# Layer 2's pairwise factor made once per pair of row tiles, in one arena of buffers

## The chip, the cores and the metric

The kernel runs on one core of one Trainium2 chip. The metric is the device time of one execution in microseconds. A core has five engines that work beside each other, each with its own queue of instructions in a fixed order: TensorE (PE, matrix products into the accumulation memory PSUM), VectorE (DVE), ScalarE (ACT, functions by tables), GpSimd (POOL) and SyncE (SP, here the issuer of DMA transfers). They meet through semaphores.

## The reference

Four graph layers run one after the other on 2708 nodes with 128 features. Each layer's output is added to its input and normalised. The change touches layer 2, a layer in hyperbolic space. Cut to what matters there:

```python
def logmap(p1, p2):
    sub = mobius_add(-p1, p2)
    sn = _norm(sub)
    return 2.0 / (sc * lambda_x(p1)) * artanh(sc * sn) * sub / sn

x = proj(x)
h = proj(mobius_matvec(W, x))
h = proj(mobius_add(h, proj(expmap0(b[None, :]))))
h_t = logmap0(h)
local_t = logmap(h[:, None, :], h[None, :, :])          # all pairs of nodes
scores = h_t @ att_wl
scores = scores[:, None] + (h_t @ att_wr)[None, :] + att_b[0]
adj_att = jax.nn.sigmoid(scores) * adj
support_t = jnp.einsum('ij,ijd->id', adj_att, local_t)
h = proj(expmap(support_t, h))
```

Each pair of nodes needs one scalar of the distance kind: with c the hyperbolic cosine of the pair's distance, the factor is arccosh(c) / sinh. This factor is the same for (i, j) and (j, i). The attention weight (sigmoid times adjacency) is not.

## The kernel before

The 2708 nodes are cut into NT = 22 row tiles of 128 (the last has 20 rows). All state lies in SBUF. Layers 0 and 1 take the time up to about 1180 us, the preparation of layer 2 to about 1242, the pairs of layer 2 from there to about 1617, then the end of layer 2 and the two adjacency products of layer 3.

The pairs are computed transposed: a unit (hf, j) has the 128 source nodes of row tile j on the partitions and half of all target nodes on the columns. There are two halves, hf = 0 with HW = 1408 columns (HT = 11 tiles) and hf = 1 with 1300. So there are 44 units, worked in the order of j, first half first. One unit goes through these steps (method names of class Pair, lines of the profile):

- load (L1330): SP brings the adjacency tile `at`. If the diagonal lies in it, POOL multiplies a 128 x 128 part by `off` to clear it (L1335).
- gram (L1337): PE makes products of the node vectors in float32 (L1343) and adds a correction of ten bfloat16 rows (L1344), 512 columns at a time into a PSUM buffer `ps`. ACT clears it into `m` (relu of minus, L1348); in every third unit DVE does this (L1346). `m` is c - 1.
- square (L1350), root (L1355), log (L1366): ACT makes u = (m + 1)^2, r = 1 / sqrt(u - 1), and later the logarithm.
- sinh (L1360), exp_d (L1363): DVE makes u = (u - 1) r, the sinh, and m = m + 1 + u, whose logarithm is the distance.
- gate (L1369), gated_adj (L1374): ACT makes the sigmoid of the scores, DVE multiplies it by `at`.
- times_d (L1377), over_sinh (L1380): DVE multiplies the distance by the gated adjacency and by r.
- add_up (L1383): PE adds the unit's part to `accV` (L1391, 128 rows) and to `accO` (L1393, one row per 512 columns, in three column groups of the array), which stay in PSUM over all 22 units of a half. After a half's last unit they are copied out. The first half's result goes to DRAM (`v_tab`) and is read again at layer 3's start, the second's stays in `VT1`.

Square and relu need no table change on ACT. Root, log and sigmoid are in three tables, so ACT loads three tables in each step.

Units go in trios, G = 3. One step of the loop handles `now` (roots, sinh, log, products), `after` (the next trio: loads, grams, squares, gates) and `done` (the previous trio: add_up). The order within a step is written out by hand under `tc.manual_schedule()`, and each engine keeps it:

```python
for v in now: v.root()
for v in now: v.gated_adj()
for v in after: v.load()
for v in now: v.sinh()
add_up(0); gram(after, 1)
for v in now: v.exp_d()
for v in after[:2]: v.square()
add_up(1); gram(after, 2)          # its clears are on DVE
for v in now: v.log()
for v in after[2:]: v.square()
for v in now: v.times_d()
for v in after: v.gate()
add_up(2); gram(trio(step + 2), 0)
for v in now: v.over_sinh()
```

The buffers come from five pools: 7 for m, 5 for u, 4 each for r, w and `at`, all of 1408 columns. Grams use a pool of four PSUM buffers.

Of the kernel before, what the change touches and what calls it, by code (L numbers as in the profile page):

```python
# [3 lines left out]

# [8 lines left out]
F32 = mybir.dt.float32  # L13
BF16 = mybir.dt.bfloat16
U32 = mybir.dt.uint32
AF = mybir.ActivationFunctionType
# [4 lines left out]
P = 128  # L21
# [18 lines left out]
def gnn_stack(ctx: ExitStack, tc: tile.TileContext, t, out: bass.AP):  # L40
# [975 lines left out]
    def layers_1_to_3(top, before_end=lambda: None):  # L1016
# [144 lines left out]
        with ExitStack() as l2:  # L1161
# [139 lines left out]
            HT = NT // 2  # L1301
            HW = HT * P
            halves = [(0, HW), (HW, N)]
            assert all(b - a <= 3 * BANK for a, b in halves)
            G = 3
            V0T = wp.tile([P, 2, BANK], F32, name="V0T")
            nc.vector.memset(V0T, 0.0)
            with ExitStack() as att:
                pm = att.enter_context(tc.tile_pool(name="pair_m", bufs=2 * G + 1))
                pu = att.enter_context(tc.tile_pool(name="pair_u", bufs=2 * G - 1))  # L1310
                pr = att.enter_context(tc.tile_pool(name="pair_r", bufs=G + 1))
                pw = att.enter_context(tc.tile_pool(name="pair_w", bufs=G + 1))
                stream = att.enter_context(tc.tile_pool(name="adj2", bufs=G + 1))
                pacc = att.enter_context(tc.tile_pool(name="ps_acc2", bufs=1, space=PSUM))
                pg = att.enter_context(tc.tile_pool(name="ps_g", bufs=4, space=PSUM))

                class Pair:

                    acc = {}

                    def __init__(self, hf, j):
                        self.hf, self.j, self.r = hf, j, rows[j]
                        self.c0, self.c1 = halves[hf]
                        self.w = self.c1 - self.c0
                        self.js = slice(j * P, j * P + self.r)

                    def new(self, pool, name):
                        return pool.tile([P, HW], F32, name=name)[:self.r, :self.w]

                    def load(self):  # L1330
                        self.at = self.new(stream, "at")
                        nc.sync.dma_start(out=self.at, in_=adjT[self.js, self.c0:self.c1])
                        if self.c0 <= self.j * P < self.c1:
                            d = self.at[:, self.j * P - self.c0:self.j * P - self.c0 + self.r]
                            nc.gpsimd.tensor_mul(d, d, off[:self.r, :self.r])  # L1335

                    def gram(self, on_vector):  # L1337

                        self.m = self.new(pm, "m")
                        for a, b in spans(0, self.w, BANK):  # L1340
                            ps = pg.tile([P, BANK], F32, name="ps")[:self.r, :b - a]
                            c = slice(self.c0 + a, self.c0 + b)
                            nc.tensor.matmul(ps, XT[:, self.js], XT[:, c], start=True, stop=False)  # L1343
                            nc.tensor.matmul(ps, aux[0][:, self.js], aux[1][:, c], start=False, stop=True)  # L1344
                            if on_vector:
                                nc.vector.tensor_scalar(self.m[:, a:b], ps, -1.0, 0.0, op0=ALU.mult, op1=ALU.max)  # L1346
                            else:
                                nc.scalar.activation(self.m[:, a:b], ps, AF.Relu, scale=-1.0)  # L1348

                    def square(self):  # L1350

                        self.u = self.new(pu, "u")
                        nc.scalar.activation(self.u, self.m, AF.Square, bias=1.0)

                    def root(self):  # L1355

                        self.r_ = self.new(pr, "r")
                        nc.scalar.activation(self.r_, self.u, AF.Abs_reciprocal_sqrt, bias=less[:self.r])

                    def sinh(self):  # L1360
                        nc.vector.scalar_tensor_tensor(self.u, self.u, LESS_ONE, self.r_, op0=ALU.add, op1=ALU.mult)  # L1361

                    def exp_d(self):  # L1363
                        nc.vector.scalar_tensor_tensor(self.m, self.m, 1.0, self.u, op0=ALU.add, op1=ALU.add)  # L1364

                    def log(self):  # L1366
                        nc.scalar.activation(self.m, self.m, AF.Ln)

                    def gate(self):  # L1369
                        self.w_ = self.new(pw, "w")  # L1370
                        nc.scalar.activation(self.w_, slB[:self.r, self.c0:self.c1], AF.Sigmoid,
                                             bias=sr[:self.r, self.j:self.j + 1])

                    def gated_adj(self):  # L1374
                        nc.vector.tensor_mul(self.w_, self.w_, self.at)  # L1375

                    def times_d(self):  # L1377
                        nc.vector.scalar_tensor_tensor(self.m, self.m, DMAX, self.w_, op0=ALU.min, op1=ALU.mult)  # L1378

                    def over_sinh(self):  # L1380
                        nc.vector.tensor_mul(self.m, self.m, self.r_)  # L1381

                    def add_up(self):  # L1383
                        first, last = self.j == 0, self.j == NT - 1
                        if first:
                            Pair.acc = (pacc.tile([P, 3 * BANK], F32, name="accV"),
                                        pacc.tile([P, BANK], F32, name="accO"))
                        accV, accO = Pair.acc
                        pieces = spans(0, self.w, BANK)
                        for a, b in pieces:  # L1390
                            nc.tensor.matmul(accV[:, a:b], X[:self.r, self.j, :], self.m[:, a:b], start=first, stop=last)  # L1391
                        for k, (a, b) in enumerate(pieces):
                            nc.tensor.matmul(accO[32 * k:32 * k + 1, :b - a], X0[:self.r, self.j:self.j + 1],  # L1393
                                             self.m[:, a:b], start=first, stop=last)
                        if last:
                            VT = VT1 if self.hf else pr.tile([P, HW], F32, name="r")[:, :self.w]
                            for k, (a, b) in enumerate(pieces):
                                copy = nc.scalar.copy if k % 2 else nc.vector.tensor_copy
                                copy(VT[:, a:b], accV[:, a:b])
                                copy(V0T[32 * k:32 * k + 1, self.hf, :b - a], accO[32 * k:32 * k + 1, :b - a])  # L1400
                            if self.hf == 0:
                                nc.sync.dma_start(out=v_tab, in_=VT)

                units = [Pair(hf, j) for hf in range(2) for j in range(NT)]
                trios = [units[n:n + G] for n in range(0, len(units), G)]

                def trio(n):
                    return trios[n] if 0 <= n < len(trios) else []

                with tc.manual_schedule():
                    for v in trio(0):
                        v.load()
                    for step in range(-1, len(trios) + 1):
                        now, after, done = trio(step), trio(step + 1), trio(step - 1)

                        def add_up(n):
                            for v in done[n:n + 1]:  # L1420
                                v.add_up()

                        def gram(vs, n):
                            for v in vs[n:n + 1]:
                                v.gram(n == 2)

                        if step < 0:
                            gram(after, 0)
                        for v in now:
                            v.root()  # L1430
                        for v in now:
                            v.gated_adj()
                        if step >= 0:
                            for v in after:
                                v.load()
                        for v in now:
                            v.sinh()
                        add_up(0)
                        gram(after, 1)
                        for v in now:  # L1440
                            v.exp_d()
                        for v in after[:2]:
                            v.square()
                        add_up(1)
                        gram(after, 2)
                        for v in now:
                            v.log()
                        for v in after[2:]:
                            v.square()
                        for v in now:  # L1450
                            v.times_d()
                        for v in after:
                            v.gate()
                        add_up(2)
                        gram(trio(step + 2), 0)
                        for v in now:
                            v.over_sinh()

# [276 lines left out]
```

## Time and profile before

| What | us |
|---|---|
| median of three runs (1917.05 to 1921.48) | 1919.34 |
| span of the profiled execution, first to last instruction | 1917.7 |
| PE busy in the whole span | 1659.6 |
| DVE busy | 1542.7 |
| ACT busy | 1132.0 |
| POOL busy | 680.1 |
| first clear of a gram, layer 2 | at 1242.6 |
| last add_up of layer 2 ends | at 1616.6 |
| start of layer 3's first adjacency product | at 1672.4 |

The profile gives one execution. Its own time outside the profiler is not given apart from the span; the median of the runs lies 1.6 us above the span. Shares over the whole span mix stages with different limits, so the stretch from 1242 to 1618 is to be read by itself. In a group a matrix product in float32 appears as two records, and the end of a record is modelled, so the pitch from one start to the next is the better price.

### The profile page before, as it was taken

The numbers are of one execution on the slowest core, as the hardware profiler recorded it, in microseconds if no ns is written. First come the engines' busy times: TensorE is split into PE (matmuls) and PEld (weight loads), VectorE is DVE, ScalarE is ACT, GpSimd is POOL, SyncE is SP. The second block draws the span as 40 slices with busy tenths as digits, with TensorE's granted clock in tenths as the row PEclk, the third lists the DMA queues.
The fourth block names the chain that finished last, engine by engine and source line by source line (L and its number), as shares of the span: only waits on it lengthen the run. The fifth ranks groups of instructions, "written<-read, shape, count | busy, mean of one in ns | idle before, by whom it ended". The sixth has DMA issues, their size and how long they took to land.

```text
span 1917.7 us, 36464 instructions
## 1 busy us (share of the span) xinstructions
PE 1659.6 (87%) x13973; PEld 949.3 (50%) x13973; DVE 1542.7 (80%) x3632; ACT 1132.0 (59%) x1581; POOL 680.1 (35%) x426
## 2 busy tenths in 40 slices
PE   5899999999999999885699996689998996199995
PEld 4666666666666666664444443322222322044542
DVE  7899999999999999986588885789999997760104
ACT  3566666667666666654344444599998994440003
POOL 5667757767766776664100000022000243000000
PEclk8899999999999999997799997779998997599997
DMA  8756566665666666443044410122222212453330
GB/s 223 161 117 148 121 140 143 132 143 119 148 127 133 146 128 142 91 103 109 1 151 149 170 63 1 61 91 91 78 80 70 98 63 120 161 203 145 139 127 31
DMA packets 218839, 223.63 MB, mean 117 GB/s; under 512 B 28389, under 2 KB 204875, under 8 KB 212067
## 3 DMA queue, kind: packets, MB, share of 16 engines
q1 hardware_dynamic: 167614, 197.53, 33.1%
q0 software_dynamic: 51040, 23.68, 10.5%
q8 instruction: 111, 1.82, 0.4%
q14 instruction: 74, 0.60, 0.1%
HBM read 213.33 MB, written 7.83 MB: 115 GB/s over the span
## 4 chain that ended last, share of the span: by engine, by line
DVE 37%; PE 32%; POOL 10%; issue 7%; ACT 7%; DMA 6%; SPq 0%; DVEq 0%; ACTq 0%; POOLq 0%
PE acc L1634 10%; POOL far L781 9%; PE lg L1098 5%; PE acc L1105 5%; DVE ix L777 5%; DMA far<-d_tab,ix 3%; DVE w L1375 3%; DVE u L1361 3%; DVE m L1364 3%; DVE W L882 3%; PE sl L817 2%; DVE extra L795 2%; DVE m L1381 2%; DVE o L739 2%; DVE m L1378 2%
## 5 line engine op out<-in xcount | busy, mean ns | idle before, releaser
L781 POOL DMA_INDIRECT far<-d_tab,ix x352 | 562.3, 1597 | 259.5 <-DVE W L882 110.8
L895 ACT ACTIVATE g<-sl 128x768 f32<-128x768 f32 x484 | 393.4, 813 | 259.0 <-PE sl L822 240.5
L817 PE MATMUL sl<-dA,S 124*128 124x153 f16 x4840 | 409.0, 232 | 10.4 <-DVE W L882 8.0
L817 PEld LDWEIGHTS <-S 124*128 124x128 f16 x4840 | 331.0, 98 | 80.0 <-issue 68.4
L833 PE MATMUL acc<-g,W 128*32 128x128 f32 x4840 | 206.2, 278 | 0.5 <-DVE W L882 0.5
L1335 POOL TENSOR_TENSOR at<-at,off 128x128 f32<-128x128 f32 (+1 forms) x22 | 71.2, 3249 | 328.8 <-DMA at<-in_adjT 301.2
L833 PEld LDWEIGHTS acc<-g,W 128*32 128x32 f32 x4840 | 140.9, 109 | 58.7 <-issue 54.6
L822 PE MATMUL sl<-s,same 50*128 50x384 f16 x968 | 162.0, 308 | 0.0
L1391 PE MATMUL accV<-m,X 128*128 128x512 f32 (+4 forms) x264 | 128.4, 628 | 33.5 <-DVE m L1381 29.1
L882 DVE TENSOR_TENSOR W<-sl,own 128x150 f32<-128x150 f32 x484 | 143.1, 299 | 14.5 <-ACT g L895 14.2
L1099 ACT ACTIVATE w<-lg,row_L_gnn_gate_bias 128x512 f32<-128x512 f32 (+1 forms) x132 | 83.5, 636 | 108.2 <-PE lg L1098 106.9
L1343 PE MATMUL ps<-XT 128*128 128x512 f32 (+4 forms) x264 | 143.9, 629 | 3.8 <-ACT m L1348 3.6
L707 DVE TENSOR_SCALAR S<-rk 124x1000 f16<-124x1000 bf16 (+1 forms) x330 | 133.4, 430 | 0.0
L777 DVE FIND_INDEX8 ix<-v,o 128x8 uint32<-128x2728 f32 x44 | 131.7, 2993 | 0.0
L316 DVE TENSOR_TENSOR g<-ps,row_L_gnn_b 128x512 f32<-128x512 f32 (+2 forms) x14 | 7.9, 574 | 148.3 <-PE ps L314 148.2
L1098 PE MATMUL lg<-qT,mT 128*128 128x512 f32 (+2 forms) x264 | 121.1, 547 | 3.6 <-ACT w L1099 3.1
L1105 PE MATMUL acc<-w,both 128*128 128x512 f32 (+2 forms) x264 | 121.2, 547 | 0.0
L795 DVE SCALAR_TENSOR_TENSOR extra<-far,v,extra 128x128 f32<-128x128 f32 x330 | 114.8, 348 | 6.3
L739 DVE SCALAR_TENSOR_TENSOR o<-ps,ar 128x496 f32<-128x496 f32 x132 | 82.4, 624 | 38.1 <-PE ps L728 31.7
L1634 PE MATMUL acc<-at,x 128*128 128x512 f32 (+2 forms) x156 | 66.2, 574 | 48.8 <-ACT x L246 48.8
L1100 DVE TENSOR_TENSOR w<-w,at 128x512 f32<-128x512 f32 (+1 forms) x132 | 82.5, 625 | 27.2 <-ACT w L1099 27.1
L1391 PEld LDWEIGHTS accV<-m,X 128*128 128x128 f32 (+1 forms) x264 | 52.1, 211 | 97.0 <-issue 57.7
(358 smaller groups left out, 2697.6 us busy)
## 6 DMA issues: line engine op xcount, KB each, us to landing
at<-in_adjT SPq DMA_DIRECT2D x42, 1354.0 KB
ar<-in_adj SPq DMA_DIRECT2D x105, 248.0 KB
far<-s_tab SPq DMA_DIRECT2D x44, 512.0 KB
at<-in_adjT SPq DMA_DIRECT2D x42, 448.0 KB
at<-in_adjT SPq DMA_DIRECT2D x21, 704.0 KB
at<-in_adjT SPq DMA_DIRECT2D x21, 650.0 KB
held<-in_adjT SPq DMA_DIRECT2D x7, 1354.0 KB
at<-in_adjT SPq DMA_DIRECT2D x21, 280.0 KB
```

Source lines behind the costliest of these rows:

```text
L777: nc.vector.max_index(ix, self.v[:, n * 8:n * 8 + 8], self.o.rearrange("p b j -> p (b j)"))
L781: nc.gpsimd.indirect_dma_start(out=self.far[n][:, k, :], out_offset=None, in_=d_tab[:, :], in_offset=bass.IndirectOffsetOnAxis(ap=self.ix[ ...
L795: nc.vector.scalar_tensor_tensor(self.extra, f, w, self.extra, op0=ALU.mult, op1=ALU.add)
L817: nc.tensor.matmul(group[c], self.S[h][:, n, c, :], dA[q][:, b, c, :], start=c % 3 == 0 and q == 0, stop=False)
L822: nc.tensor.matmul(out, same[p], self.s3[p, :e - a, :], start=False, stop=True)
L833: nc.tensor.matmul(self.acc[q:q + 32, k, :], W[:, c, :], g[:, c, :], start=b == 0 and k == 0, stop=ends)
L882: nc.vector.tensor_tensor(W[:, :, :RG].rearrange("p (k c) i -> p k c i", k=2), columns_of(sl, D, DA), own[:, None, None, :].to_broadcast([ ...
L895: nc.scalar.activation(g.rearrange("p (k c) d -> p k c d", k=2), columns_of(sl, 0, D), AF.Gelu, scale=1.0 / D_SCALE)
L1098: nc.tensor.matmul(lg, mT[:, j * P:j * P + r], qT[:, a:b], start=True, stop=True)
L1105: nc.tensor.matmul(acc[k], mrow[:rows[j], j, :], ws[j][:rows[j], a:b], start=j == 0, stop=j == NT - 1)
L1391: nc.tensor.matmul(accV[:, a:b], X[:self.r, self.j, :], self.m[:, a:b], start=first, stop=last)
L1634: nc.tensor.matmul(acc[k], src[:rows[j], j, :], at[:rows[j], a:b], start=j == order[0], stop=j == order[-1])
```

## The change

The 44 units are put into four groups. A is hf = 0 with j = 0 to 10, B is hf = 0 with j = 11 to 21, C is hf = 1 with j = 11 to 21, and D is hf = 1 with j = 0 to 10. The factor f = distance / sinh of a unit is now made apart from the gate.

- In A and C, whose rows and columns are the same half, a unit makes f only for the columns from its own tile on (`dw` columns). The `mw` columns ahead of it are mirrored: PE transposes the blocks of the earlier units' f into PSUM (`mirror`), and DVE multiplies the gated adjacency by it there.
- B makes all of its f and also stores it in DRAM (`f_tab`). D makes none: `load_f` reads the transposed arrangement of blocks from `f_tab`, in runs of 128 numbers, and PE transposes them.
- What is added up is now `w_` (the gate, times adjacency, times f) and no longer `m`.
- All clears of grams are on ACT.
- All SBUF buffers of the stage lie in one arena of 264 blocks of 128 columns, as many as the five pools had. A small allocator, run when the program is built, chooses the blocks: the shortest free run that fits, and among those the one released longest ago. A unit's f is given back column block by column block.
- There are 14 steps of two to five units, and the order within a step is a different one.

```diff
+            f_tab = dram.tile([HT, P, HW], F32, name="f_tab")
...
-                pm = att.enter_context(tc.tile_pool(name="pair_m", bufs=2 * G + 1))
-                pu = att.enter_context(tc.tile_pool(name="pair_u", bufs=2 * G - 1))
-                pr = att.enter_context(tc.tile_pool(name="pair_r", bufs=G + 1))
-                pw = att.enter_context(tc.tile_pool(name="pair_w", bufs=G + 1))
-                stream = att.enter_context(tc.tile_pool(name="adj2", bufs=G + 1))
+                CELLS = 264
+                arena = att.enter_context(tc.tile_pool(name="arena", bufs=1)).tile([P, CELLS * P], F32, name="arena")
...
+                def taken(width):
+                    n, runs = -(-width // P), []
...
+                    fits = [(len(r), max(free[k] for k in own), own[0]) for r in runs if len(r) >= n
+                            for own in (r[:n], r[-n:])]
+                    at = min(fits)[2]
...
+                        self.own_half = self.c0 <= j * P < self.c1
+                        self.first = j - hf * HT if self.own_half else 0
+                        self.mw = self.first * P if self.own_half else self.w if hf else 0
+                        self.dw = self.w - self.mw
...
+                    def load_f(self):
+                        if self.dw == 0:
+                            at = taken(HW)
+                            self.cells["f"] = set(range(at, at + HT))
+                            f = self.fT = arena[:, at * P:at * P + HW].rearrange("p (k c) -> p k c", c=P)
+                            k = HT - 1
+                            nc.sync.dma_start(out=f[:, :k, :], in_=f_tab[:k, :, self.js].rearrange("k p c -> p k c"))
+                            nc.sync.dma_start(out=f[:rows[-1], k, :], in_=f_tab[k, :rows[-1], self.js])
...
                     def over_sinh(self):
-                        nc.vector.tensor_mul(self.m, self.m, self.r_)
+                        nc.vector.scalar_tensor_tensor(self.f, self.u, DMAX, self.f, op0=ALU.min, op1=ALU.mult)
+                        self.drop("u")
+                        if not self.own_half:
+                            nc.sync.dma_start(out=f_tab[self.j - HT, :self.r, :], in_=self.f)
+
+                    def times_f(self):
+                        v = self.w_[:, self.mw:]
+                        nc.vector.tensor_mul(v, v, self.f)
...
+                    def mirror(self, a, b):
+                        ps = pg.tile([P, BANK], F32, name="ps")[:self.r, :b - a]
+                        for c in range(a, b, P):
+                            k = c // P
...
+                            nc.tensor.transpose(ps[:, c - a:c - a + n], src, ident[:n, :n])
+                        nc.vector.tensor_tensor(self.w_[:, a:b], self.w_[:, a:b], ps, op=ALU.mult)
...
+                A, B = [Pair(0, j) for j in range(HT)], [Pair(0, j) for j in range(HT, NT)]
+                C, D_ = [Pair(1, j) for j in range(HT, NT)], [Pair(1, j) for j in range(HT)]
+                steps = [A[:2], A[2:5], A[5:7] + B[:1], A[7:8] + B[1:3], A[8:9] + B[3:5], A[9:10] + B[5:7],
+                         A[10:] + B[7:9], B[9:], C[:2] + D_[:1], C[2:4] + D_[1:3], C[4:6] + D_[3:5], C[6:8] + D_[5:7],
+                         C[8:] + D_[7:9], D_[9:]]
...
+                        for v in direct(now):
                             v.root()
+                        for v in done:
+                            for a, b in v.mirrors:
+                                v.mirror(a, b)
+                            if v.dw:
+                                v.times_f()
+                        add_up()
+                        clears(4)
+                        for v in direct(now):
+                            v.sinh()
+                            v.exp_d()
+                        per = -(-len(grams) // max(1, len(adds)))
+                        while adds:
+                            add_up()
+                            clears(per)
+                        clears(len(grams))
+                        for v in direct(now):
+                            v.log()
                         for v in now:
                             v.gated_adj()
+                        for v in after:
+                            v.load()
                         for v in after:
                             v.gate()
+                        for v in direct(now):
+                            v.over_sinh()
                         for v in now:
-                            v.over_sinh()
+                            v.load_f()
+                        coming = [(v, a, b) for v in direct(at_step(step + 2)) for a, b in v.direct]
+                        early = [v.gram(a, b) for v, a, b in coming[:2]]
```

`direct(vs)` are the units with dw > 0. `clears(n)` takes the next n gram pieces of the coming step: it issues the piece's products on PE unless they were issued early, clears it on ACT, and after a unit's last piece squares it on ACT. Two pieces of the step after are issued early at the end of a step.

## The prediction

> **What bounds the kernel now.** I first looked for the stage that the change touches, then for what ends last in one of its steps. The busy time by stretch comes first; columns are length, then busy time and count for PE, weight loads, DVE, ACT and POOL, then clock, DMA share and GB/s.
>
> ```profile
> core 0: us, PE busy (x) PEld busy (x) DVE busy (x) ACT busy (x) POOL busy (x), PEclk, DMA share, GB/s
> 1353.40:1378.00 24.60, 22.08 (x64) 6.89 (x63) 24.60 (x19) 22.87 (x22) 0.00 (x0) 1.00 0.26 88
> 1526.50:1549.40 22.90, 20.97 (x64) 6.96 (x63) 22.90 (x20) 21.71 (x22) 8.65 (x3) 1.00 0.26 88
> 1242.00:1618.00 376.00, 338.67 (x925) 108.02 (x924) 354.01 (x270) 333.45 (x319) 69.56 (x19) 0.91 0.22 75
> ```
>
> The pairs take 376 of 1917.7 us. In a step of three tiles DVE has no gap, but PE and ACT are within 3 us of it: less DVE work alone gains little. The chain of waits over one step is DVE from end to end, three tiles of 1408 columns in 4.61 us an operation:
>
> ```profile
> 1352.95 3.14 DVE m L1381 x2
> 1356.09 4.61 DVE w L1375 x3
> 1360.70 4.61 DVE u L1361 x3
> 1365.30 4.61 DVE m L1364 x3
> 1369.91 1.67 DVE m L1346 x3
> 1371.57 4.60 DVE m L1378 x3
> ```
>
> ACT and PE prices are read from the timeline:
>
> ```profile
> 1355.16 1.28 ACT L1358 ACT_TABLE_LOAD   x1
> 1356.46 4.19 ACT L1358 ACTIVATE r<-u,less 128x1408 f32<-128x1408 f32 x3
> 1361.88 2.65 ACT L1353 ACTIVATE u<-m 128x1408 f32<-128x1408 f32 x2
> ...
> 1353.08 2.63 PE L1391 MATMUL accV<-m,X 128*128 128x512 f32 x6 [0.82 <-DVE m L1381]
> 1355.64 1.03 PE L1393 MATMUL accO<-m,X 128*1 128x512 f32 x6
> 1356.59 1.12 PE L1343 MATMUL ps<-XT 128*128 128x512 f32 x2
> 1357.65 0.38 PE L1344 MATMUL ps<-aux,aux 10*128 10x512 bf16 x1
> 1357.96 1.13 PE L1343 MATMUL ps<-XT 128*128 128x512 f32 x2
> ...
> 1592.30 4.70 PE L1391 MATMUL accV<-m,X 128*128 128x512 f32 x6 [6.42 <-DVE m L1381]
> 1596.93 1.61 PE L1393 MATMUL accO<-m,X 128*1 128x512 f32 x6
> ```
>
> One add-up is 1353.08 to 1356.59, 3.51 us (3.33 at 1300 columns); a gram of 512 columns 1.37. The last two lines show an add-up after PE waited 6.42 us: it takes some 2.8 us longer.
>
> Prices for w columns in thousands, fitted through the 1408 and 1300 forms: DVE 0.07 + 1.04w; ACT square and log 0.155 + 0.83w, root and gate 0.23 + 0.83w, a clear 0.06 + 0.83w, a table 1.285; a gram piece 0.29 + 2.09w.
>
> [...]waits of 1.3 to 6.4 us were mostly followed by 1.6 to 2.8 us more on the add-up; two waits, of 1.9 and 2.5 us, were not. [...]here 273 ns, but 21 of them pass in 2.42 us at 1239.72, so I take 0.13. [...]the clears from PSUM (1.67 for 1408 columns) run at the SBUF rate already, so a mirror product is priced at 0.10 + 1.04w. [...]the smallest adjacency load (104 KB) landed in 2.4.
>
> **The change, part by part.** Sums over tiles: widths are 1408 for the first half, 1300 for the second, 59,576 columns in 44 tiles. Made directly are 8,448 (A) + 15,488 (B) + 7,260 (C) = 31,196; mirrored 28,380, in 69 pieces with 231 transposes.
> - DVE: removed are five passes over 59,576 and 42 clears, 325 + 24 = 349. It keeps one full pass (65), four direct ones (139) and gets the mirror products (36): about 241.
> - ACT: three functions and the clears fall to 31,196 columns, DVE's clears come to it, gates stay, tables fall from 45 to about 40: 332 becomes some 240.
> - PE: grams fall from 163 to 87 (75 pieces for 132), add-ups stay at 150, transposes bring 30: 267 at full clock, where 316 were.
> - DMA: B's tiles are stored (11 of 704 KB) and returned as 512-byte runs (11 of 665 KB), on SP's queue.
> - The arena has the old pools' 264 blocks; its selection rule only decides which past reader a new buffer waits for.
>
> So every engine gets some 50 to 100 us less work. What sets the time is the order. In the new step ACT's logs stand behind all clears of the next tiles, PE issues the last grams behind the third add-up, and the add-ups need the products, which need over_sinh, which needs the logs. Before, the last tile's clear was on DVE and its square behind the logs, so this ring was open. Now it is closed once a step. Laid out for the step with A8, B3, B4 (A7, B1, B2 being added up, A9, B5, B6 coming), from one last log to the next: over_sinh of B2 1.53; mirror and product of A7 1.73 (its transposes are early); add-up 3.51; grams 512 and 384, 2.45 (two more were early); add-up 3.51; two grams 2.73; add-up 3.51; gram 1.09; last clear 0.38; square 1.32; table 1.285; logs 3.12. That is 26.2, and 0.1 for each of some six hand-overs (product to accV took 0.13) makes 26.7, against 24.69 before. During the logs PE has two early grams and seven transposes, so it waits about 6 us, longer than the waits that slowed it before: 2.0 more, 28.7.
>
> The same sum for the steps after the first gives 21.7, 25.2, 26.3, 26.2, 26.1, 24.7, 23.3 and 17.9, together 191.4, with hand-overs 196. The ramp to the first logs is ACT's own 9.2 + 17.7 and some 1.6 of waits for grams: 28.5. So the logs of the first second-half step (C0, C1, D0) end at 224.5.
>
> From there D decides. D's load is the last thing in its step, and I followed its buffer through the allocator's rule in the diff: D0's, D1's and D3's were last read by an over_sinh of the same step, and D2 and D4 are queued behind them. So these loads start when the step is over, while all transposes stand ahead of the first add-up on PE. An adjacency tile takes 1.9 (four of 704 KB were released 1.77 apart), a D tile 2.7 (the load of x, also 512-byte runs, moved 203 GB/s at a share of 0.82, so 250 at most)[...].
> - C0/D0 to C2/C3: over_sinh done 3.1 after the log, D0 3.8 later, its transposes 1.9, add-up 3.3, grams 2.0, clear and square 1.1, table 1.3, logs 1.9: 18.4.
> - C2/C3 to C4/C5: 3.1, two D loads behind adjacency loads 10.0, transposes 1.8, add-up 3.3, gram 1.1, then 3.9: 23.2.
> - to C6/C7: 2.9 + 10.9 + 1.9 + 3.3 + 3.1 = 22.1.
> - to C8/C9/C10: SP stands at C9's adjacency load, whose buffer waits for the step's last add-up (7.2 after the log); then four adjacency loads, D5 and D6 15.5, transposes 1.5, table and logs 2.6: 26.8.
> - to the end: PE alone, four add-ups 13.3, transposes paced by DVE 7.5 (less what lies in the logs), five add-ups 16.7, transposes 2.9, two add-ups 6.7: 44.3 with the overlap taken off.
>
> Sum: 224.5 + 18.4 + 23.2 + 22.1 + 26.8 + 44.3 = 359.3. Cold PE: 2.0 in six steps of the first half and twice in the second, 16: 375. The clock of this sum starts a gram before the first clear (1242.61), at 1241.2: the last add-up ends at 1616.5, and before it ended at 1616.6. The stage is level.
>
> Around it: the second half's closing tile is read back through DRAM into space that the arena holds until the end, so that load (before issued at 1609.6, used at 1620.1) now lands some 4.1 after the last add-up where 3.5 was allowed: 0.6 to 1.5 more, I take 1.5. Adjacency loads no longer start at 1202 but when the arena is free, near 1242; they are wanted 20 us later, so nothing. [...]Stores of f lie beside other traffic (88 GB/s moved): nothing, and 2 us if D0 waits for the last.
>
> Against its own span the profiled execution gains nothing and loses about 1.5. The median of the three runs, 1919.3, lies 1.6 above that span, so about 1921.
>
> **Bounds of the unknown.** Cold PE: 0 (it stays warm) to 26 (2.8 in nine places; below nothing is excluded, waiting can't speed it). D's rate: 125 to 400 GB/s, +18 to -5. Hand-overs at 0.06 or 0.18: -2 to +6. Transposes at 0.273 instead of 0.13, on the path in the last three steps only: +10; at 0.10, -2.
>
> **Rivals.**
> - PE stays warm: some waits of 2.5 us left no trace. Then 359, some 15 less: 1905. Against: the waits are about 6 us now, and no wait over 2.6 was free before.
> - The engines' sums rule, as in the trace before, where DVE was never late: the largest of each step's three sums, added up, is 292, so 1242 to 1540, about 1845 to 1880 with part of the ring left. It needs the logs not to stand behind the clears; the timeline speaks for a kept order (log at 1369.94, then square, table, gate as written).
> - Slower: D's loads at half the rate, in the four steps that wait for them. 512-byte runs picked out of 5.6 KB rows, beside adjacency loads and f's stores, at 125 GB/s: one load is 5.4, seven of them stand on the path, 2.7 each, 19: 1940. It decides from about 200 GB/s down. For: 1.3 MB of such runs a step; against: x's load.
> - The change doesn't keep tiles apart: if waits went by the whole arena, not by columns, every write would wait for every earlier read and steps would run engine after engine, 40 us and more each, over 2050. Against: X, one buffer, is scaled by ACT and DVE tile by tile while PE transposes earlier ones (1221 to 1230).
>
> **How the numbers follow.** Chances: level, 0.42 (1912 to 1931); warm PE 0.16; sums rule 0.09; slow D 0.25; whole arena 0.08. The likeliest gives 1921; its own range is 1912 to 1931. Leaving out the sums and the whole arena, 0.17, the range is 1897 to 1945. A measurement here tells 0.2%, 3.8 us. Of the level case 0.11 lies below, 0.18 within, 0.13 above. Faster 0.11 + 0.16 + 0.09 = 0.36; same 0.18; slower 0.13 + 0.25 + 0.08 = 0.46.
>
> **What would show it.** In the changed profile: DVE and ACT some 240 us busy in the stage and PE about 300 with the cold part; idle PE ahead of accV once a step, released by DVE, 5 us or more; steps of 26 to 29 us in the first half; in the second, transposes that wait for a load of f; the last add-up near 1617. Steps of 20 to 22 us, logs ahead of the clears, or D's loads landing within a step would make it wrong.

## The result and the profile after

The changed kernel takes 1918.43 us (median of 20 runs, 1916.53 to 1922.31), the kernel before 1919.43 in the same series. The ratio is 0.9997 with a 95% interval of 0.999 to 1.0004: no change. The span of the profiled execution is 1918.0 us.

The first view is the busy time by stretch of the changed kernel. The columns are those of the same view before: length, busy time and count of PE, weight loads, DVE, ACT and POOL, then PE's granted clock (1.00 is full), DMA share, GB/s.

```profile
1378.20:1405.40 27.20, 22.16 (x65) 7.64 (x65) 20.22 (x18) 20.53 (x23) 0.46 (x1) 0.88 0.42 146
1242.00:1618.00 376.00, 300.75 (x980) 118.55 (x978) 251.95 (x252) 243.90 (x264) 16.47 (x23) 0.84 0.35 119
```

In the same 376 us DVE is now busy 252 us where it was 354, ACT 244 where it was 333, PE 301 where it was 339. So the work went, as the change says, and none of it became time. In a step of the first half (first line) no engine is full. The step takes 27.2 us where a trio took 24.7.

The next view is the chain of waits of the changed kernel over that step: start, length, and what ran. L1426 is over_sinh, L1464 and L1466 are add_up, L1386 a gram, L1396 its clear, L1414 the logs.

```profile
1379.76 1.62 DVE arena L1426
1382.03 4.07 PE accV L1464 x6
1386.10 0.96 PE accO L1466 x4
1387.06 1.05 PE ps L1386 x2
1389.54 2.56 PE accV L1464 x6
...
1395.80 2.56 PE accV L1464 x6
1398.36 0.96 PE accO L1466 x4
...
1400.46 0.50 ACT arena L1396
...
1402.36 1.28 ACT L1414
1403.98 1.37 ACT arena L1414
1405.37 1.30 DVE arena L1426
```

Before, this chain was DVE alone. Now it goes round: over_sinh, the first mirror product, three add-ups with grams between them, the last gram, its clear and square on ACT, the logs, over_sinh. Such a closed path is called a ring below. The timeline of the same step shows who waits at each corner; the brackets give the idle time of the engine ahead of the instruction and what ended it.

```profile
1382.03 4.07 PE L1464 MATMUL accV<-arena,X 128*128 128x512 f32 x6 [5.90 <-DVE arena L1450]
...
1400.46 0.49 ACT L1396 ACTIVATE arena<-ps 128x384 f32<-128x384 f32 x1 [4.02 <-PE ps L1387]
1400.98 1.38 ACT L1400 ACTIVATE arena<-arena 128x1408 f32<-128x1408 f32 x1
...
1402.36 1.28 ACT L1414 ACT_TABLE_LOAD   x1
...
1403.65 2.95 ACT L1414 ACTIVATE arena<-arena 128x256 f32<-128x256 f32 x3
1404.10 0.42 DVE L1426 SCALAR_TENSOR_TENSOR arena<-arena 128x256 f32<-128x256 f32 x1 [4.86 <-ACT arena L1414]
```

PE stands 5.90 us, ACT 4.02 us for the last gram, DVE 4.86 us for the logs. Each waits for the next. The first add-up after PE's wait takes 4.07 us on its accV part, the later ones 2.63 (2.56 in the chain, which counts from the end of the instruction before). The granted clock over that wait and the add-up shows why; the last two lines are a stretch of the kernel before, with a wait of 1.26 us and the add-up behind it:

```profile
1374.73:1378.14 3.41, 1.41 (x10) 0.94 (x9) 0.56 (x1) 3.39 (x5) 0.46 (x1) 1.00 1.00 416
1378.14:1384.97 6.83, 2.94 (x4) 1.38 (x5) 6.75 (x7) 6.80 (x7) 0.00 (x0) 0.50 0.76 281
1384.97:1388.38 3.41, 3.41 (x13) 0.78 (x12) 2.22 (x4) 3.40 (x4) 0.46 (x1) 1.00 0.47 190
...
1499.18:1502.59 3.41, 2.15 (x7) 0.78 (x6) 3.41 (x4) 3.40 (x3) 0.00 (x0) 1.00 0.01 2
1502.59:1506.00 3.41, 3.41 (x5) 1.35 (x4) 3.41 (x3) 3.38 (x6) 0.00 (x0) 0.50 0.00 0
```

The clock is halved in the middle of the wait and full again at 1384.97, 2.9 us into the add-up.

The second half has another picture. This is the timeline of the changed kernel at the start of the step that adds up C2, C3, D1 and D2. L1380 is the load of f, L1449 the transposes.

```profile
1500.39 2.52 DVE L1426 SCALAR_TENSOR_TENSOR arena<-arena 128x1044 f32<-128x1044 f32 x2
...
1502.98 0.38 SPq L1380 DMA_DIRECT2D arena<-f_tab  x1
...
1503.99 0.77 PE L1449 MATMUL ps<-ident,arena 128*128 128x128 f32 x5
...
1504.87 0.41 SPq L1380 DMA_DIRECT2D arena<-f_tab  x1
...
1509.80 5.08 PE L1449 MATMUL ps<-ident,arena 128*128 128x128 f32 x22 [5.04 <-DMA arena<-f_tab]
...
1514.81 2.45 PE L1464 MATMUL accV<-arena,X 128*128 128x512 f32 x6
```

The load of D1 is issued 0.07 us after over_sinh has ended (1500.39 + 2.52). By the allocator's rule its buffer holds columns that this over_sinh read last, and the load is the next piece in the chain of waits. PE waits for it and starts the first add-up at 1514.81, 11.9 us after over_sinh. PE's clock is at half until 1514.68: the 22 transposes take 5.08 us, where 22 take 2.88 us at 1608.13.

The ends agree: the last add-up ends at 1616.6 before and at 1617.6 now, layer 3's first product starts at 1672.4 and at 1673.1.

### The profile page after: what moved, and what is told of

It reads as the page before. It is cut to its first block, busy times and chain, and to the rows that moved or that the text cites. A ratio compares the mean times of both kernels' runs of the same rounds, so it can differ in the third digit from the quotient of the medians.

```text
span 1918.0 us, 36613 instructions
## 1 busy us (share of the span) xinstructions
PE 1620.9 (85%) x14033; PEld 960.8 (50%) x14033; DVE 1441.5 (75%) x3615; ACT 1041.9 (54%) x1528; POOL 624.7 (33%) x426
## 4 chain that ended last, share of the span: by engine, by line
PE 41%; DVE 29%; POOL 8%; DMA 8%; issue 7%; ACT 6%; SPq 0%; DVEq 0%; ACTq 0%; POOLq 0%
PE acc L1726 10%; POOL far L782 8%; PE accV L1464 6%; PE lg L1099 5%; PE acc L1106 5%; DVE ix L778 5%; DMA far<-d_tab,ix 4%; DVE W L883 3%; DVE extra L796 2%; PE ps L1386 2%; PE accO L1466 2%; DVE o L740 2%; PE sl L818 2%; DVE S L708 2%; DVE dA L701 2%
## 5 line engine op out<-in xcount | busy, mean ns | idle before, releaser
L834 PEld LDWEIGHTS acc<-g,W 128*32 128x32 f32 x4840 | 140.6, 109 | 58.7 <-issue 55.5
L1464 PE MATMUL accV<-arena,X 128*128 128x512 f32 (+4 forms) x264 | 130.4, 636 | 20.9 <-DVE arena L1450 11.8
L1372 POOL TENSOR_TENSOR arena<-arena,off 128x128 f32<-128x128 f32 (+1 forms) x22 | 16.3, 741 | 344.2 <-DMA arena<-in_adjT 264.7
L1464 PEld LDWEIGHTS accV<-arena,X 128*128 128x128 f32 (+1 forms) x264 | 54.1, 219 | 89.0 <-issue 61.4
L747 DVE MAX8 cand<-o 128x8 f32<-128x248 f32 x242 | 90.4, 411 | 0.0
```

The costliest lines, as they stand in the source:

```text
L834: nc.tensor.matmul(self.acc[q:q + 32, k, :], W[:, c, :], g[:, c, :], start=b == 0 and k == 0, stop=ends)
L1464: nc.tensor.matmul(accV[:, a:b], X[:self.r, self.j, :], self.w_[:, a:b], start=first, stop=last)
```

## The experiments

All ratios, and the us less or more, are against the kernel before, in the same series of runs. Each edit is to the changed kernel, whose own time is within 0.1% of it; only the last run's is to the kernel with both edits.

**Logs first.** The prediction's reason for the first half was that ACT's logs stand behind the last clears. This run moves only the logs.

```diff
                         while adds:
                             add_up()
+                            if not adds:
+                                for v in direct(now):
+                                    v.log()
                             clears(per)
-                        clears(len(grams))
-                        for v in direct(now):
-                            v.log()
+                        if len(done) < 2:
+                            clears(len(grams))
+                            for v in direct(now):
+                                v.log()
```

> One order is changed in the changed kernel: ACT's logs stand ahead of the clears that follow the step's last add-up. Theory (the ring over log, over_sinh, product, three add-ups, last grams, last clear and square sets the first half, 27.2 us a step measured): those last grams, the clear and the square leave the ring, steps of the first half fall to 21 to 23 us, about 30 us in all: 1880 to 1895. Rival (the first half is held by something else, such as the arena's buffers, and only D's loads matter): within 5 us of the changed kernel's 1918. The second half should not move by more than 5 us under either.

Measured: 1882.14 us, ratio 0.9804 (0.9788 to 0.9821), 36.8 us less than the 1918.95 of before in that series. The timeline of this kernel in one step of the first half:

```profile
1350.92 1.28 ACT L1414 ACT_TABLE_LOAD   x1
1352.22 3.06 ACT L1414 ACTIVATE arena<-arena 128x384 f32<-128x384 f32 x3
...
1355.18 0.47 ACT L1396 ACTIVATE arena<-ps 128x384 f32<-128x384 f32 x1
1355.68 1.38 ACT L1400 ACTIVATE arena<-arena 128x1408 f32<-128x1408 f32 x1
...
1358.91 2.63 PE L1464 MATMUL accV<-arena,X 128*128 128x512 f32 x6 [1.04 <-DVE arena L1450]
```

The logs now run while PE makes the last gram, whose clear comes behind them. PE's wait ahead of the first add-up falls from 5.90 to 1.04 us, and with it goes the slow add-up. The first adds of two neighbouring steps are at 1337.68 and 1358.91, 21.2 us apart. So the ring set the first half. The last gram, its clear and the square no longer lie on it. The second half still waits as before: its first two waits for loads of f are 6.34 and 5.12 us here, 6.07 and 5.04 in the changed kernel.

**Loads of f earlier.** In the second half the candidate was the place of D's loads, at the end of their step.

```diff
                         add_up()
+                        for v in now:
+                            v.load_f()
                         clears(4)
...
-                        for v in now:
-                            v.load_f()
```

> D's loads of f are issued after the first add-up of their own step and no longer at its end, so that their buffers were last read a step earlier; nothing else is moved. Theory (the transposes of D wait for these loads, and every add-up is queued behind them): the waits of 5 to 8.5 us for loads of f go, 15 to 25 us in all: 1893 to 1903, first half unchanged. Rival (PE is full in the second half anyway, its waits only take the place of waits for DVE): under 6 us.

(The edit lies directly behind the first add-up.) Measured: 1901.01 us, ratio 0.991 (0.9893 to 0.9926), 17.9 us less. The timeline of this kernel at the start of the step that adds up C2, C3, D1 and D2:

```profile
1490.43 0.38 SPq L1380 DMA_DIRECT2D arena<-f_tab  x1
...
1491.49 0.38 SPq L1380 DMA_DIRECT2D arena<-f_tab  x1
...
1500.78 0.77 PE L1449 MATMUL ps<-ident,arena 128*128 128x128 f32 x5
...
1504.97 2.88 PE L1449 MATMUL ps<-ident,arena 128*128 128x128 f32 x14 [0.96 <-DVE arena L1450]
...
1507.78 3.33 PE L1464 MATMUL accV<-arena,X 128*128 128x512 f32 x6
```

Both loads are issued some 10 us ahead of the transposes, and no transpose waits for DMA longer than 0.2 us. What is left are waits of 1 us for DVE, which frees the PSUM buffers of the transposes. By the allocator's rule D1's buffer was now last read by C0's add-up, and not, as expected, a step earlier: that add-up ends at 1490.38, 0.05 us ahead of the load. What counts is that this reader is done early in the step. From the first transposes to the first add-up it is now 7.0 us; in the changed kernel it was 10.8 (1503.99 to 1514.81). The early loads also changed which buffers other loads find, so the adjacency load that stood behind a late add-up is gone too; the two are not told apart here.

**PE kept busy.** The add-up after a wait is slow. Does that lie on the ring? This run fills the wait with products that are made over again into the same buffer (`gram` takes that buffer as a third argument here).

```diff
                         early = [v.gram(a, b) for v, a, b in coming[:2]]
+                        if 0 <= step < 7:
+                            v, a, b = coming[0]
+                            for _ in range(3):
+                                v.gram(a, b, early[0])
```

> At the end of the steps 0 to 6 PE makes the first early gram three times more into the same buffer, about 4 us of work that changes nothing, in the wait ahead of the first add-up. Theory (that wait lets PE's clock fall, the first add-up takes 4.1 instead of 2.6 us, and this lies on the ring): about 1.5 us a step, 8 to 11 us faster than the changed kernel, 1908 to 1910. Rival (the slow add-up is hidden): no change; if the added products delay the transposes, slower by up to 7.

Measured: 1908.32 us, ratio 0.9946 (0.993 to 0.9963), 10.6 us less, with more work done. In the timeline of this kernel (accV is L1465 here) the repeated products fill the wait where they are long, and the first add-up is then quick. Where the repeated piece is short, the wait and the slow add-up stay:

```profile
1375.84 4.71 PE L1465 MATMUL accV<-arena,X 128*128 128x512 f32 x6 [4.17 <-DVE arena L1451]
...
1403.79 2.53 PE L1465 MATMUL accV<-arena,X 128*128 128x512 f32 x6
...
1427.67 2.53 PE L1465 MATMUL accV<-arena,X 128*128 128x512 f32 x6
```

The mean granted clock of this run's profiled execution is 0.928, that of the changed kernel's 0.919. So the slow PE after a wait is a part of the ring's length, not hidden.

**Long runs.** The rival for the second half was the form of D's loads, 1300 runs of 512 bytes each.

```diff
-                            k = HT - 1
-                            nc.sync.dma_start(out=f[:, :k, :], in_=f_tab[:k, :, self.js].rearrange("k p c -> p k c"))
-                            nc.sync.dma_start(out=f[:rows[-1], k, :], in_=f_tab[k, :rows[-1], self.js])
+                            nc.sync.dma_start(out=arena[:, at * P:at * P + HW], in_=f_tab[self.j % 10])
```

> D's loads read one stored tile as it lies, 128 runs of 5632 bytes, and not the blocks that they need in 1300 runs of 512 bytes; so D's part of the output is made from other numbers, in the same amount of work. Theory (a load of f costs by its place in the queue and by its waits, and by its short runs only 0.7 to 1.5 us each): 2 to 7 us faster than the changed kernel. Rival (the short runs are what makes these loads slow): 15 us or more faster.

Measured: 1915.13 us, ratio 0.9981 (0.9974 to 0.9989), 3.8 us less. The edit also drops the small second load, so the 3.8 us are the most that the form of the runs can be worth here; the place of the loads is worth almost five times as much.

**Both edits.** Logs first and loads early, together.

> The two edits together: logs ahead of the last clears, and D's loads of f issued after the first add-up of their step. If the ring and the loads are two separate costs, one in each half, the gains add up: 36.8 and 17.9 off 1918.9, so 1862 to 1867. If they share a resource (ACT or the store and load traffic), less: 1870 or more.

Measured: 1863.73 us, ratio 0.9715 (0.9699 to 0.9731), 55.7 us less, where the two gains alone make some 55. They are two separate costs. The busy time by stretch of this kernel, whose pairs end some 57 us earlier than in the kernel before:

```profile
1242.00:1562.00 320.00, 286.67 (x982) 109.07 (x982) 250.01 (x253) 243.91 (x265) 18.82 (x23) 0.91 0.41 141
1290.00:1430.00 140.00, 130.58 (x417) 45.42 (x415) 126.36 (x109) 129.98 (x137) 8.03 (x8) 0.98 0.42 154
1480.00:1562.00 82.00, 78.23 (x360) 35.91 (x358) 49.36 (x79) 31.91 (x40) 2.54 (x6) 1.00 0.42 133
```

In the first half all three engines are now over 90% busy, in the second PE alone.

**Add-up between the transposes.** With both edits in place, the first add-up was taken out from behind the third and later units' transposes.

```diff
-                        for v in done:
+                        for n, v in enumerate(done):
+                            if n == 2:
+                                add_up()
                             for a, b in v.mirrors:
                                 v.mirror(a, b)
...
-                        add_up()
+                        if len(done) <= 2:
+                            add_up()
```

> As the kernel with both edits, and the first add-up of a step is issued between the transposes of the second and the third unit that is added up, no longer behind all of them. Theory (with the loads early, PE still waits for the pacing of the transposes by two free PSUM buffers, 2 to 3 us in each of the second half's steps): 4 to 10 us faster than with both edits. Rival (DVE then waits for the transposes behind the add-up, and its chain is what the next step needs): no change or up to 8 us slower.

Measured: 1864.55 us, ratio 0.9719 (0.97 to 0.9739), against 1863.73 without this edit: no change, so the gain of 4 to 10 us did not come. The trace of the kernel with both edits shows that less was left to gain than expected: PE is busy for 78.23 of the 82.00 us, and its waits for DVE among the transposes come to 2.1, 1.5, 0.8 and 0.4 us in the last four of the second half's steps, where 2 to 3 were expected in each. In the profiled executions the pairs end at 1557.2 with this edit and at 1559.5 without; these 2.3 us don't show in the medians of four and five runs. Whether the rival's reason, DVE's chain, holds is not shown.

## Why the prediction was right

It named the level case as the likeliest, 1921 us, and 1918.4 was measured. The steps, one by one:

- **Less work on every engine: right.** About 241, 240 and 267 us at full clock were worked out for DVE, ACT and PE. DVE and ACT measure 252 and 244 over the stage, which includes the copies at the ends of the halves. PE's 301 include 75 us of busy time at half clock (the same view taken over those stretches). An accV that lies wholly at half clock takes 5.06 us (at 1273.28), one at full clock 2.63; by this ratio the 75 would be 39, which makes 265, an estimate. (By the prediction's own prices PE had 313 before, not 316: 163 of grams and 150 of add-ups. Its 665 KB for a load of f are 650 in the unit in which the stored tile is 704.)
- **The ring through the logs: right, and shown** by moving the logs alone. For the step laid out, 28.7 us were predicted and 27.2 measured. Two terms were too large. The mirror and product of 1.73 us ahead of the add-up: accV takes its 512 columns as soon as these are multiplied, and it starts 0.74 us after DVE's first product (1381.29 to 1382.03). And the slow PE was put at 2.0 us for this step; it was 1.4 (4.07 against 2.63).
- **PE's clock after the wait: right in sum, shown** by keeping PE busy; what halves the clock stays open. 16 us in eight places were assumed. In the trace of after the first accV of eleven steps is slow, by 0.6 to 2.4 us, about 19 in all, and transposes after a long wait are slow too (22 in 5.08 us at 1509.80, 2.88 at 1608.13), which the prediction left out. In the steps of 27.2 us PE had run 21 us without a long gap before it stood for 5.9 us, and paid 1.4; the largest cost, 2.4, came after waits of 2.7 and 6.2 us. So the length of the wait alone does not say the price. In the trace of after, each of the 112 stretches of 3.413 us from 1241.61 to 1623.90 has a mean clock of 1.00 or 0.50 and nothing between, so the clock changed only where one of them ends; the halved ones at 1350.84 and 1378.14 start 27.30 us, eight stretches, apart. The add-up at 1382.03 is slow until its stretch ends at 1384.97. Before, the clock was halved at 1502.59 after a stretch in which PE was busy for 2.15 of 3.41 us, and it stayed full over a wait of 2.52 us ahead of 1377.77. What decides between these two is open.
- **D's loads at the end of their step: right, and shown** by issuing them earlier, for three of the four steps. The mirror products were expected to be done 11.8 us after over_sinh in the step that adds up D1 and D2; its first add-up starts at 11.9. The step that adds up D3 and D4 was also to wait for its loads, and takes 23.0 us from log to log where 22.1 were laid out. But no transpose waits for DMA there; the chain goes through PE's add-ups and the mirror products. That this number fits is luck.
- **The rate of D's loads: the slower rival did not come.** With long runs only 3.8 us are saved. How much of a load's price does not grow with its size was not shown. The step that waits for D5 and D6 was even priced too high: from the last add-up of the step before (1553.5) to the next one 17.0 us were laid out, 15.5 until both loads are there and 1.5 for transposes. The first transpose of D5 is at 1563.9 and the add-up at 1568.9, after 15.4.
- **The reading back of the first half's tile, 1.5 us: too high.** The trace of after shows PE waiting for it only 0.91 us at 1622.05, and from the last add-up to layer 3 it is 55.5 us as against 55.8 before.

The two halves hold each by itself. The prediction's first half, with 12 us of slow PE, ends with logs at 1477.7, and these end at 1479.1; from there to the last add-up 138.8 us were laid out and 138.5 measured. Single steps missed by 2 to 3 us either way: from the logs of C0 and C1 to those of C2 and C3 it took 21.0 us and not 18.4 (the load of D0 took 6.4 us from issue to use where 3.8 were laid out), to the logs of C8 to C10 25.1 and not 26.8. So the mechanism was right, and that the sum is right to about 1 us is partly luck. The rival in which the engines' sums rule was wrong for this order, but it is where the kernel with both edits goes: there the pairs end near 1560, still 20 us above that sum's 1540. The rival in which PE stays warm did not come either, but its 15 us were a fair price: filling the waits of a part of the first half's steps brings 10.6, and the ring stays. Dependencies by the whole arena, the last rival, are excluded by the 0.07 us between over_sinh and the load that waits for its columns, with the other engines at work on the arena.

What stays open: how much of the 17.9 us of the early loads belongs to the adjacency load that stood behind an add-up. No run kept one and moved the other. In the trace of after that load stands in SP's queue until the add-up ends at 1553.5, some 6 us; by this estimate from one wait, most of the gain belongs to the place of the loads of f themselves.

## What to carry to other kernels

Work taken off the busiest engine is worth nothing if the new order closes a ring over several engines: follow one step from a result to the same result one step later, through every queue position, and compare that length with the engines' sums. An instruction that starts such a path must not stand in its queue behind one that waits for the path's end; moving three lines of logs was worth 37 us here. When buffers come from one space, look at who last read the blocks that a load gets, and issue the load where that reader is done early.

## What was not expected of the hardware

- Issuing the small second part of a load of f (20 rows of one block, L1381) held SP for 0.6 to 1.4 us in six of eleven cases, but for 2.9 to 3.3 us three times right behind another load of f (once for only 1.8) and once behind a row of adjacency loads. What makes the difference is not shown.
- POOL's 22 multiplications by `off`, which share nothing in the program with what DVE does at that time, took 0.45 us at the median in both kernels. Before, with DVE busy without a gap, five took 7.7 to 8.6 us and the last, of only 20 x 20, took 19.0; now none took over 1.81. What made them long is not shown.
- Transposes of 128 x 128 in float32 passed every 0.13 us in a row (22 in 2.88 us), though each is recorded with some 0.27 (the 273 ns of the prediction), and every 0.23 at half clock (22 in 5.08 us).
- PE's granted clock rose at 1514.68 after PE had made nothing but transposes since 1509.80 (22 in 5.08 us). At 1569.29 it did not rise after nearly the same work (22 in 5.13 us from 1563.86).
